# Layer 0 of a two-layer graph network for pairs of batches: a second level of seven-product blocking, and an order of all engines over two batches

## The chip, the core and the metric

The kernel runs on one core of one Trainium2 chip, in fp32 throughout. The time is the device time of one execution in microseconds (us); lower is better. A core has five engines with a queue each: TensorE (PE; its weight loads are PEld), VectorE (DVE), ScalarE (ACT), GpSimd (POOL) and SyncE (SP), which here issues nearly all DMAs.

## The reference

For each of 64 batches, x is 256 x 512 and adj is 256 x 256. Two layers follow each other, each with a residual and a layer norm:

```python
deg = jnp.sum(adj, axis=-1, keepdims=True)
agg = jnp.einsum('bij,bjf->bif', adj, x) / jnp.maximum(deg, EPS)
out = jnp.einsum('bnf,of->bno', jnp.concatenate([x, agg], axis=2), W)
x = _layernorm(x + relu(out))                          # layer 0
...
q, k, v = (proj(Wq, bq), proj(Wk, bk), proj(Wv, bv))   # 8 heads of 64
scores = einsum('bhqd,bhkd->bhqk', q, k) * SCALE * (adj + adj)[:, None]
ctx = einsum('bhqk,bhkd->bhqd', softmax(scores), v)
x = _layernorm(x + (ctx @ Wo.T + bo))                  # layer 1
```

## The kernel before, in words

**Seven products instead of eight.** The large products are done as 2 x 2 blocks by the Strassen-Winograd scheme. `winograd` (L408) makes the steps of one: products 5, 1, 3, 6, 2, 7, 4 into three PSUM accumulators a, b and c; "kept" steps that copy a partial sum out while the accumulator goes on accumulating; "joined" steps that add an accumulator to what was kept. The left blocks are sums of tokens that POOL makes (`token_sums`, L381), the right ones sums of weights made once at the start (`weights`, L239). So layer 0's product with both halves of W ("L": L1 to L7 are the products, Lk the copies on ACT at L464, Lj the joins on DVE at L429), Q and K together ("Q", L475 and L491), V ("V") and the output projection ("O"; keep_o, L516, adds `rest` on the way). L, V and O multiply at L448. A product of L is two fp32 matmuls of 128x128 weights and 512 columns: the 256 columns of both halves of W (m = 0 and 1), for two blocks of the contraction (c = 0 and 1). In the trace each fp32 matmul leaves two records.

**The stages of a batch.** x and adj come in turned layouts (Dzx, Dza) and as rows (Dx, Dadj). DVE transposes 32 x 32 blocks of the turned ones (xT0, xT1, aT; L354). L gives `oy`: half 0 is x W0, half 1 is x W1; then adj times half 1 by the seven-product scheme ("Y", lone 128x256 matmuls at L571, with aS and bS sums on POOL at L553), scaled by the degree and added (Yk, Yj; L593), relu and residual (AYr), layer norm (AYb on DVE, AYp on POOL, AYn on ACT). The result goes to DRAM (Dway), comes back turned (Dz1) and is transposed (x1T, L639), and once more as rows (`rest`, Drest) to which POOL adds the bias (bo).

**Attention.** For each of four pairs of heads a to d: scores (S, L674), multiplied by the mask by DVE from PSUM (m, L687), the row maximum (M, L697), exponential with the sum (e and f, ACT, L703), reciprocal (r), normalization (n, ACT, L720), a block transpose (T, DVE, L727), a way through DRAM (Dw, L732, into ws; Ds, L741, back into sT), contexts (C0a, C0b, C1a, C1b; L757), copies of them (c0, c1), O, and the last norm (lb, lp, ln) and output (Dout) from tile h1.

**Buffers.** SBUF tiles have one buffer each but for a few: zx, za and z (of step Dz1) are tiles of their own; sa to sd and sTa to sTd are eight tiles; xS, yS, cS, aS and yB hold four sums each. All PSUM accumulators rotate through eight banks of 128x512.

**The order.** Nothing is scheduled by a compiler: the steps are emitted in the order of three lists written out, START, PLAN and END, and every engine executes its own steps in that order. PLAN is one turn for one batch: "L1+2" is step L1 of the batch two ahead. Batches overlap over several turns.

## Time and profile before

| | |
|---|---|
| median of 3 runs | 3069.9 us (3069.35 to 3070.3) |
| the profiled execution | 3068.5 us, its span 3066.7 us, TensorE clock 0.998 |
| busy share of the span: PE, PEld, DVE, ACT, POOL | 99%, 76%, 70%, 55%, 42% |
| instructions: PE, DVE, ACT, POOL | 17552, 3914, 4995, 2189 |
| moved by DMA | 513.45 MB, 167 GB/s |

The span runs from the first to the last instruction of the execution that was profiled; the time beside it is that execution's own. A busy share is the part of the span in which at least one instruction of the engine was running; consecutive instructions overlap somewhat, so what one occupies is read from the distance between two starts. The row of a group of instructions gives busy time, mean duration, and what ended the idle time before it.

### The profile page before, as it was taken

How to read it: one execution, taken by the hardware profiler on the slowest of the kernel's cores; microseconds unless marked ns; L12 is line 12 of the kernel's file. 1: busy time of each engine (PE TensorE's matmuls, PEld its weight loads, DVE VectorE, ACT ScalarE, POOL GpSimd, SP SyncE). 2: the span in 40 equal slices, each digit the busy share in tenths (PEclk: the TensorE clock that was granted, in tenths of full speed). 3: DMA queues.
4: the chain of work that ended last, by engine and by line, in shares of the span. 5: the costliest groups of instructions: out<-in, count | busy, mean ns of one | idle time of the engine just before them, and what ended most of it. 6: DMA issues, size and time to landing. Idle time of an engine off the chain costs nothing.

```text
span 3066.7 us, 53019 instructions
## 1 busy us (share of the span) xinstructions
PE 3030.1 (99%) x17552; PEld 2323.7 (76%) x17552; DVE 2144.6 (70%) x3914; ACT 1689.7 (55%) x4995; POOL 1288.0 (42%) x2189
## 2 busy tenths in 40 slices
PE   7999999999999999999999999999999999999997
PEld 5778778777787787777877877778778777787785
DVE  5767777776777777777777677767776777676775
ACT  2655555555555556555555565555555555555565
POOL 4434444443444444434444444344444443444433
PEclk9999999999999999999999999999999999999999
DMA  8576566566675665665756656657666566576656
GB/s 175 134 183 177 154 179 175 152 183 166 158 182 153 178 172 154 179 168 155 186 152 178 172 154 177 173 151 185 159 172 172 155 182 171 151 184 162 165 144 173
DMA packets 494112, 513.45 MB, mean 167 GB/s; under 512 B 113808, under 2 KB 392336, under 8 KB 493840
## 3 DMA queue, kind: packets, MB, share of 16 engines
q1 hardware_dynamic: 493264, 509.02, 63.2%
q8 instruction: 141, 2.31, 0.3%
q10 hardware_dynamic: 576, 1.05, 0.1%
q14 instruction: 131, 1.07, 0.1%
HBM read 308.55 MB, written 201.33 MB: 166 GB/s over the span
## 4 chain that ended last, share of the span: by engine, by line
PE 97%; DMA 2%; DVE 1%; ACT 0%; SPq 0%; issue 0%; POOL 0%; POOLq 0%; DVEq 0%; ACTq 0%
PE Qa L475 15%; PE La L448 15%; PE Qc L475 7%; PE pc L757 7%; PE Oa L448 7%; PE Lc L448 7%; PE Va L448 7%; PE Qb L475 4%; PE Ya L571 4%; PE Lb L448 4%; PE Oc L448 4%; PE Vc L448 4%; PE Ycb L571 3%; PE scd L674 2%; PE Ob L448 2%; PE Vb L448 2%
## 5 line engine op out<-in xcount | busy, mean ns | idle before, releaser
L491 ACT ACTIVATE qk<-Qa,bqk 128x128 f32<-128x128 f32 x768 | 217.8, 364 | 518.3 <-PE Qa L475 518.3
L529 POOL TENSOR_SCALAR mv<-mv 128x1 f32<-128x1 f32 x256 | 76.9, 301 | 773.7 <-DVE mv L524 760.1
L464 ACT COPY oy<-La 128x512 f32<-128x512 f32 x192 | 112.6, 586 | 383.7 <-PE La L448 383.6
L389 POOL TENSOR_TENSOR yS<-x1T 128x256 f32<-128x256 f32 x128 | 94.2, 737 | 427.0 <-DVE x1T L639 426.3
L389 POOL TENSOR_TENSOR cS<-cT 128x256 f32<-128x256 f32 x128 | 90.9, 731 | 347.5 <-ACT cT L773 347.5
L516 DVE TENSOR_TENSOR h<-Oa,rest 128x256 f32<-128x256 f32 x192 | 81.5, 424 | 155.2 <-PE Oa L448 149.0
L720 ACT ACTIVATE sc<-sc,totalc 128x256 f32<-128x256 f32 x256 | 109.2, 498 | 106.4 <-DVE totalc L715 106.4
L653 POOL TENSOR_TENSOR rest<-rest,bo_sb 128x512 f32<-128x512 f32 x128 | 160.5, 1278 | 13.3 <-DMA rest<-way 13.3
L703 ACT ACTIVATE sd<-sd,nmaxd 128x256 f32<-128x256 f32 x256 | 127.0, 497 | 66.7 <-DVE nmaxd L697 66.7
L506 ACT COPY v<-Va 128x256 f32<-128x256 f32 x192 | 71.2, 371 | 158.2 <-PE Va L448 158.2
L727 DVE STREAM_TRANSPOSE sd<-sd 128x1024 f32<-128x1024 f32 x64 | 79.6, 1244 | 110.2 <-ACT sd L720 110.2
L530 POOL TENSOR_TENSOR mv<-mv,neg_half 128x1 f32<-128x1 f32 x256 | 144.9, 566 | 21.4
L553 POOL TENSOR_TENSOR yB<-oy 128x256 f32<-128x256 f32 x128 | 94.6, 739 | 131.7 <-DVE oy L429 126.4
L475 PEld LDWEIGHTS Qa<-x1T,Wq 128*128 128x128 f32 x1024 | 124.3, 192 | 28.2 <-issue 27.3
L429 DVE TENSOR_TENSOR oy<-Lb,oy 128x512 f32<-128x512 f32 x64 | 44.2, 690 | 141.9 <-PE Lb L448 135.2
L448 PE MATMUL Lb<-W,xT 128*128 128x512 f32 x256 | 122.2, 600 | 15.1 <-DMA W<-in_w0t_dram 15.1
L703 ACT ACTIVATE sa<-sa,nmaxa 128x256 f32<-128x256 f32 x256 | 127.0, 499 | 5.2 <-DVE nmaxa L697 5.2
L703 ACT ACTIVATE sb<-sb,nmaxb 128x256 f32<-128x256 f32 x256 | 126.3, 496 | 3.6 <-DVE nmaxb L697 3.6
L475 PEld LDWEIGHTS Qa<-x1T,Wq_sums 128*128 128x128 f32 x1024 | 124.2, 192 | 4.3 <-issue 1.1
L703 ACT ACTIVATE sc<-sc,nmaxc 128x256 f32<-128x256 f32 x256 | 126.4, 496 | 1.1 <-DVE nmaxc L697 1.1
L475 PEld LDWEIGHTS Qa<-yS,Wq 128*128 128x128 f32 x1024 | 124.2, 192 | 3.6 <-issue 0.5
L475 PEld LDWEIGHTS Qc<-yS,Wq_sums 128*128 128x128 f32 x1024 | 124.3, 192 | 3.3
(167 smaller groups left out, 8926.7 us busy)
## 6 DMA issues: line engine op xcount, KB each, us to landing
zx<-in_x_dram SPq DMA_DIRECT2D x256, 128.0 KB, 3.0
x<-in_x_dram SPq DMA_DIRECT2D x256, 128.0 KB, 3.5
way<-x SPq DMA_DIRECT2D x64, 512.0 KB, 3.2
z<-way SPq DMA_DIRECT2D x256, 128.0 KB, 2.8
rest<-way SPq DMA_DIRECT2D x64, 512.0 KB, 4.7
wsa<-sa SPq DMA_DIRECT2D x64, 512.0 KB, 5.6
wsc<-sc SPq DMA_DIRECT2D x64, 512.0 KB, 3.0
sTc<-wsc SPq DMA_DIRECT2D x256, 128.0 KB, 3.8
```

The costliest lines, as they stand in the source:

```text
L389: nc.gpsimd.tensor_tensor(part_of(s, b, [P, 4, 2, P])[:, k], left(b), right(b), op)
L448: nc.tensor.matmul(ps[:, :width].rearrange("p (m o) -> p m o", o=G), lhsT=left(k, b, c), rhs=w(WEIGHTS[k])[:, :, c], start=first and c == ...
L464: nc.scalar.copy(part_l(b, t, n), ps.rearrange("p (m o) -> p m o", m=2))
L475: nc.tensor.matmul(ps.rearrange("p (m j q) -> p m j q", m=2, j=2)[:, m, j], lhsT=wqk(WEIGHTS[k])[:, m, c, j * P : (j + 1) * P], rhs=left_y ...
L491: nc.scalar.activation(part_q(b, t, n)[:, m, j], ps.rearrange("p (m j q) -> p m j q", m=2, j=2)[:, m, j], AF.Identity, bias=bqk[:, m, c : ...
L530: nc.gpsimd.tensor_tensor(mv[:, 1:2], mv[:, 1:2], neg_half, ALU.pow)
L553: steps[f"{name}{k}"] = lambda b: nc.gpsimd.tensor_tensor(of(k)(b), left(b), right(b), op)
L571: nc.tensor.matmul(ps[:, G:] if acc == "b" else ps[:, :G], lhsT=left(b), rhs=right(b), start=k in (5, 1), stop=True, skip_group_check=True,)
L653: nc.gpsimd.tensor_tensor(rest, rest, bo_sb, ALU.add)
L703: nc.scalar.activation(rows(b)[:, r], rows(b)[:, r], AF.Exp, bias=of("nmax", b)[:, r : r + 1], accum_out=of("total", b)[:, r : r + 1],)
L720: nc.scalar.activation(rows(b)[:, r], rows(b)[:, r], AF.Identity, scale=of("total", b)[:, r : r + 1])
L757: nc.tensor.matmul(ps[j * D : (j + 1) * D, hp % 2], lhsT=held["v", b][:, c, h * D : (h + 1) * D], rhs=held[f"sT{name}", b][:, :, c, j * NT ...
```

## The change

- Layer 0 is done for two batches together. Each block product of L, except the second, becomes a 2 x 2 scheme of its own, over the two batches (beta), the two blocks of the contraction (c) and the two halves of W (m): seven unit products of 128x256 ("L51" is unit 1 of block product 5) instead of two times two matmuls of 512 columns. Product 2 stays as it was, once a batch (step L2).
- The left sides of the units are sums on POOL (Ls, four of 128x128 for each block product and pair), the right sides sums of weights made once (W0i, six times four sums of 128x256 on DVE).
- Each unit has its own "Le" step that takes its accumulator into `oy`: 42 a pair, of which eight are copies on ACT and 34 additions on DVE. The sums among the block products that accumulators held before are made by Lj2 and by La12 and La22, additions of 128x512 on POOL.
- The mask step m becomes four fused instructions that multiply and take the row maximum; M becomes a negation of four values on POOL.
- SBUF is rearranged: zx, za and z share one tile "z"; Ds brings the turned scores back into sa to sd themselves; `rest` serves in place of h1; chains of sums keep two tiles instead of four and overwrite the first; xT, oy, v and others have a tile for even and one for odd batches.
- START, PLAN and END are new; a turn is two batches. The start of PLAN, its middle, and the core of the rest of the diff:

```diff
+    Sa+0 Le62+2 Dx+2 Sb+0 Ls31+2 ma+0 La12+2 Sc+0 Dza+3 Sd+0 Ls72+2 mb+0 Ma+0 Ls74+2 fa+0 C1a-1 Ls33+2
+    C1b-1 mc+0 Mb+0 Ls32+2 Ls34+2 c1-1 L75+2 yS3+1 L71+2 fb+0 O2-1 Le71+2 cS1-1 Le75+2 L31+2 md+0 Mc+0
+    L76+2 bo-1 ec+0 L72+2 L73+2 O5-1 Le31+2 ea+0 Le76+2 L35+2 L36+2 Le35+2 cS2-1 O1-1 eb+0 Le36+2 cS3-1
+    Le73+2 L33+2 Ok1-1 L37+2 fc+0 Ok5-1 L77+2 Le37+2 O6-1 Ls41+2 Le33+2 Md+0 Le77+2 L32+2 yS1+1 ed+0
+    Le72+2 L45+2 rb+0 cS4-1 L74+2 Oj2-1 Y1+2 Ok6-1 aS1+2 rc+0 nb+0 L34+2 Le74+2 Ls43+2 O3-1 Le34+2 bS1+2
+    Le32+2 L42+2 La22+2 Oj3-1 O7-1 ra+0 lb0-1 na+0 Y5+2 bS3+2 Q5+1 Yk1+2 Tb+0 aS2+2 Ls42+2 fd+0 bS2+2
+    L41+2 Q1+1 Le41+2 La22+3 nc+0 Oj7-1 Ta+0 aS3+2 O4-1 Ls44+2 Yk5+2 Dwa+0 Y6+2 Qk1+1 Le45+2 Dwb+0 V5+1
...
+    AYr0+2 V6+1 AYb0+2 Q7+1 Vk5+1 yS4+1 Vk6+1 Dzx+4 Yk4+2 AYp0+2 AYr1+2 V7+1 Dsc+0 AYb1+2 aS3+3 AYn0+2
+    bS1+3 Q3+1 lb1-1 ln0-1 AYp1+2 Dsd+0 Qj7+1 V3+1 lp1-1 Le47+2 AYn1+2 Qj3+1 Q4+1 Vj3+1 Dway+2 ln1-1
+    Vj7+1 Dout-1 L44+2 Qk4+1 V4+1 Le44+2 xT0+4 Sa+1 Vk4+1 Qj2+1 Sb+1 xT1+4 Dz1+2 C0a+0 C1a+0 ma+1 C0b+0
+    Drest+0 C1b+0 c0+0 mb+1 Ma+1 c1+0 Sc+1 ea+1 cS1+0 Sd+1 mc+1 aS1+3 V2+1 fa+1 bS3+3 Mb+1 Y5+3 x1T+2
+    cS3+0 O2+0 eb+1 bS2+3 Y1+3 Dzx+5 O5+0 Mc+1 Yk1+3 aS2+3 fc+1 md+1 yS1+2 Q2+2 Dx+3 cS2+0 fb+1 Y6+3
+    Dadj+5 Y2+3 Yk6+3 aS4+3 ec+1 O1+0 Yk5+3 yS3+2 ra+1 Q5+2 Vj2+1 bo+0 Yj2+3 na+1 Y3+3 Y7+3 Yj3+3 Qk5+2
+    V5+2 bS4+3 rc+1 Ok5+0 xS1+4 Yj7+3 Q1+2 Ok1+0 nc+1 xS3+4 xT0+5 Oj2+0 O6+0 rb+1 Ta+1 V1+2 cS4+0 xT1+5
...
-FIRST_TURN = 3
-LAST_TURNS = 4
+FIRST_TURN = 2
+LAST_TURNS = 2
...
+    OUTER = {1: B11, 2: B21, 3: B22, 4: T4, 5: T1, 6: T2, 7: T3}
+    SPLIT = (1, 5, 6, 7, 3, 4)
+    w0_inner = const.tile([P, len(SPLIT), 3, G], F32, name="W0_inner")
+    def inner_weights(k):
+        unit = lambda c, m: w0(OUTER[k])[:, m, c]
+        t1, t2, t4 = (w0_inner[:, SPLIT.index(k), n] for n in range(3))
+        return {1: unit(0, 0), 2: unit(1, 0), 3: unit(1, 1), 4: t4, 5: t1, 6: t2, 7: unit(0, 1)}
+    def sum_inner_weights(k):
+        w = inner_weights(k)
+        @step(f"W0i{k}")
+        def _(_):
+            for dst, a, b in ((5, 7, 1), (6, 3, 5), (7, 3, 7), (4, 2, 6)):
+                nc.vector.tensor_tensor(w[dst], w[a], w[b], ALU.subtract)
...
+    def staged(name, b):
+        return part_of(name, b, [P, NT * F], tag="z")
...
-        z = tile_of("zx", b, [P, A, NT, F // A])
+        z = staged("zx", b).rearrange("p (b t k) -> p b t k", b=A, t=NT)
...
-        z = tile_of("za", b, [P, A, NT, N // A])
+        z = staged("za", b)[:, : NT * N].rearrange("p (b t k) -> p b t k", b=A, t=NT)
...
+    def x_turned(b):
+        return part_of("xT", b, [P, FC, NT, P], tag=f"xT{b % 2}")
...
+    def chain_sums(s, engine, place, block):
+        def put(k, left, right, op):
+            steps[f"{s}{k}"] = lambda b: engine.tensor_tensor(place(b, k == 3), left(b), right(b), op)
+        put(1, lambda b: block(b, 1, 0), lambda b: block(b, 1, 1), ALU.add)
+        put(2, lambda b: place(b, 0), lambda b: block(b, 0, 0), ALU.subtract)
+        put(3, lambda b: block(b, 0, 0), lambda b: block(b, 1, 0), ALU.subtract)
+        put(4, lambda b: block(b, 0, 1), lambda b: place(b, 0), ALU.subtract)
...
+        def place(b, n):
+            return part_of(s, b, [P, 2, 2, P])[:, n]
+        chain_sums(s, nc.gpsimd, place, block)
+        return lambda k, b, c: (block(b, *BLOCK[k]) if k in BLOCK else place(b, k == 7))[:, c]
...
-    def part_l(b, t, n):
-        return part_of("oy", b, [P, 2, NT, F])[:, :, t, n * G : (n + 1) * G]
-    def keep_l(b, ps, t, n):
-        nc.scalar.copy(part_l(b, t, n), ps.rearrange("p (m o) -> p m o", m=2))
-    winograd("L", right_weights(token_sums("xS", "xT"), w0, F), keep_l, part_l)
+    def oy_block(b, m, t, n):
+        return part_of("oy", b, [P, 2, NT, F], tag=f"oy{b % 2}")[:, m, t, n * G : (n + 1) * G]
...
+    def x_sum(b, n):
+        return part_of("xS", b - b % 2, [P, 2, 2, 2, P])[:, n, b % 2]
+    chain_sums("xS", nc.gpsimd, x_sum, x_block)
+    def split_product(k):
+        def unit(b, beta, c):
+            return (x_block(b + beta, *BLOCK[k]) if k in BLOCK else x_sum(b + beta, k == 7))[:, c]
+        def unit_sum(b, n):
+            return part_of(f"xs{k}", b, [P, 4, P], tag=f"xs{SPLIT.index(k) % 2}")[:, n - 1]
+        for n, left, right, op in (
+            (1, lambda b: unit(b, 1, 0), lambda b: unit(b, 1, 1), ALU.add),
+            (2, lambda b: unit_sum(b, 1), lambda b: unit(b, 0, 0), ALU.subtract),
+            (3, lambda b: unit(b, 0, 0), lambda b: unit(b, 1, 0), ALU.subtract),
+            (4, lambda b: unit(b, 0, 1), lambda b: unit_sum(b, 2), ALU.subtract),
+        ):
+            small_sum(f"Ls{k}", n, lambda n: lambda b: unit_sum(b, n), left, right, op)
+        w = inner_weights(k)
+        lefts = {q: lambda b, q=q: unit(b, *BLOCK[q]) for q in BLOCK}
+        lefts |= {q: lambda b, n=n: unit_sum(b, n) for q, n in ((5, 1), (6, 2), (7, 3), (3, 4))}
+        def accumulator(q, b):
+            name = f"L{k}a" if q in (1, 6, 7, 4) else f"L{k}cb"
+            ps = bank(name, b) if (name, b) not in held else held[name, b]
+            return ps[:, G:] if q == 2 else ps[:, :G]
+        def product(q):
+            @step(f"L{k}{q}")
+            def _(b):
+                nc.tensor.matmul(
+                    accumulator(q, b), lhsT=lefts[q](b), rhs=w[q], start=q in (5, 1), stop=True, skip_group_check=True
+                )
+        t, n = {5: (1, 1), 3: (0, 1)}.get(k, (1, 0))
+        def taken(q, beta, m):
+            @step(f"Le{k}{q}")
+            def _(b):
+                dst, ps = oy_block(b + beta, m, t, n), accumulator(q, b)
+                if k in (1, 5) and q in (5, 1, 6, 4):
+                    nc.scalar.copy(dst, ps)
+                else:
+                    nc.vector.tensor_tensor(dst, ps, dst, ALU.add)
+        for q in (5, 1, 3, 6, 2, 7, 4):
+            product(q)
+        for q, beta, m in ((5, 1, 1), (1, 0, 0), (6, 0, 1), (4, 1, 0), (3, 0, 1), (2, 0, 0), (7, 1, 1)):
+            taken(q, beta, m)
...
+    def both(b, t, n):
+        oy_block(b, 0, t, n)
+        return held["oy", b][:, :, t, n * G : (n + 1) * G]
+    @step("L2")
+    def _(b):
+        ps = bank("L2", b).rearrange("p (m o) -> p m o", m=2)
+        for c in range(2):
+            nc.tensor.matmul(ps, lhsT=x_block(b, 0, 1)[:, c], rhs=w0(B21)[:, :, c], start=c == 0, stop=c == 1)
+    @step("Lj2")
+    def _(b):
+        ps = held["L2", b].rearrange("p (m o) -> p m o", m=2)
+        nc.vector.tensor_tensor(both(b, 0, 0), ps, both(b, 1, 0), ALU.add)
+    @step("La12")
+    def _(b):
+        nc.gpsimd.tensor_tensor(both(b, 0, 1), both(b, 1, 0), both(b, 1, 1), ALU.add)
+    @step("La22")
+    def _(b):
+        nc.gpsimd.tensor_tensor(both(b, 1, 1), both(b, 1, 1), both(b, 1, 0), ALU.add)
...
-        return part_of("h1", b, [P, NT, F])[:, t, n * G : (n + 1) * G]
+        return held["rest", b][:, t, n * G : (n + 1) * G]
     def keep_o(b, ps, t, n):
-        rest = held["rest", b][:, t, n * G : (n + 1) * G]
-        nc.vector.tensor_tensor(part_o(b, t, n), ps[:, :G], rest, ALU.add)
+        nc.vector.tensor_tensor(part_o(b, t, n), ps[:, :G], part_o(b, t, n), ALU.add)
...
-        return lambda b: part_of("yB", b, [P, 4, G])[:, k - 1]
+        return lambda b: part_of("yB", b, [P, 2, G])[:, k == 3]
...
-        z = tile_of("z1", b, [P, NT, A, P])
+        z = staged("z1", b).rearrange("p (t b k) -> p t b k", t=NT, b=A)
...
-            tile_of(f"s{name}", b, [P, A, NT, R, L])
+            s = tile_of(f"s{name}", b, [P, A, NT, R, L])
+            nmax = tile_of(f"nmax{name}", b, [P, R], small, "nmax")
             for j in range(2):
-                nc.vector.tensor_tensor(
-                    rows(b)[:, j * NT : (j + 1) * NT],
-                    sc(b, j).rearrange("p t (k l) -> p t k l", l=L),
-                    held["adj", b].rearrange("p t (k l) -> p t k l", l=L),
-                    ALU.mult,
-                )
+                for t in range(NT):
+                    r = j * NT + t
+                    nc.vector.tensor_tensor_reduce(
+                        out=s[:, :, :, r],
+                        in0=sc(b, j)[:, t].rearrange("p (a c l) -> p a c l", a=A, l=L),
+                        in1=held["adj", b][:, t].rearrange("p (a c l) -> p a c l", a=A, l=L),
+                        scale=1.0,
+                        scalar=-3.4028234663852886e38,
+                        op0=ALU.mult,
+                        op1=ALU.max,
+                        accum_out=nmax[:, r : r + 1],
+                    )
         @step(f"M{name}")
         def _(b):
-            nmax = tile_of(f"nmax{name}", b, [P, R], small, "nmax")
-            nc.vector.tensor_reduce(nmax, rows(b), AX.XY, ALU.max, negate=True)
+            nc.gpsimd.tensor_scalar(of("nmax", b), of("nmax", b), -1.0, None, ALU.mult)
...
-            sT = tile_of(f"sT{name}", b, [P, A, NT, R, L])
             for a, part in groups():
                 nc.sync.dma_start(
-                    out=sT[part].rearrange("l b c r m -> l b (c r m)"),
+                    out=of("s", b)[part].rearrange("l b c r m -> l b (c r m)"),
...
-    turn = [(name[:-2], int(name[-2:])) for name in PLAN.split()]
...
-        for i in range(FIRST_TURN, B - LAST_TURNS):
+        for i in range(FIRST_TURN, B // 2 - LAST_TURNS):
             for name, ahead in turn:
-                run(name, i + ahead)
+                run(name, 2 * i + ahead)
```

## The prediction

> **What bounds the kernel now.** I read the page first: busy time by engine and the shares of the chain that ended last.
>
> ```profile
> PE 3030.1 (99%) x17552; PEld 2323.7 (76%) x17552; DVE 2144.6 (70%) x3914; ACT 1689.7 (55%) x4995; POOL 1288.0 (42%) x2189
> PE 97%; DMA 2%; DVE 1%; ACT 0%; SPq 0%; issue 0%; POOL 0%; POOLq 0%; DVEq 0%; ACTq 0%
> ```
>
> TensorE is on the chain for 97% of the span. To see whether it ever waits in the steady part, the view of waits on PE from 200 to 2866 us, which has two rows in all:
>
> ```profile
> PE pc L757 <- DMA sTb<-wsb: 1.3, 1, 1.3
> PE pc L757 <- DMA sTd<-wsd: 0.6, 1, 0.6
> ```
>
> So 1.9 us in 2666: any TensorE time taken out is time saved, as long as no other engine becomes late. The cycle of one batch, from one start of the scores of heads d to the next, is a row of the view of busy time by stretch (sum columns PE, PEld, DVE, ACT, POOL):
>
> ```profile
> 1526.41:1573.49 47.08, 47.08 (x275) 36.26 (x274) 33.27 (x62) 26.32 (x78) 19.90 (x35) 1.00 0.61 166
> ```
>
> A pair of batches is 94.16 us of TensorE; beside it DVE has 66.5 us of work, ACT 52.6, POOL 39.8. What an instruction occupies is read from starts, not durations, since matmuls overlap. PE's timeline:
>
> ```profile
> 1514.48 0.59 PE L571 MATMUL Ya<-yB,aS 128*128 128x256 f32 x2
> 1514.91 0.59 PE L571 MATMUL Ycb<-oy,aS 128*128 128x256 f32 x2
> 1515.34 1.03 PE L448 MATMUL Vc<-Wv_sums,yS 128*128 128x256 f32 x4
> ...
> 2897.42 1.88 PE L448 MATMUL Lc<-W_sums,xS 128*128 128x512 f32 x4
> 2899.13 1.88 PE L448 MATMUL La<-W_sums,xS 128*128 128x512 f32 x4
> ```
>
> A lone 128x256 product (two records) takes 0.433 us, with weights of its own and a semaphore of its own; a block product of layer 0 (two of 128x512) takes 1.717. The same way: a Q product 1.785, a V or O product 0.865, four scores or contexts 0.865. DVE's timeline gives its spacing:
>
> ```profile
> 1501.58 0.41 DVE L516 TENSOR_TENSOR h<-Oc,rest 128x256 f32<-128x256 f32 x1
> 1501.91 0.41 DVE L429 TENSOR_TENSOR h<-Ob,h 128x256 f32<-128x256 f32 x1
> 1502.24 0.17 DVE L715 RECIPROCAL totala<-totala 128x4 f32<-128x4 f32 x1
> ...
> 1531.23 1.28 DVE L687 TENSOR_TENSOR sa<-sca,adj 128x512 f32<-128x512 f32 x2
> 1532.42 1.27 DVE L687 TENSOR_TENSOR sb<-scb,adj 128x512 f32<-128x512 f32 x2
> ...
> 1533.73 1.22 DVE L697 TENSOR_REDUCE nmaxb<-sb 128x4 f32<-128x1024 f32 x1
> 1534.87 1.21 DVE L697 TENSOR_REDUCE nmaxa<-sa 128x4 f32<-128x1024 f32 x1
> ```
>
> 128x256 with a PSUM operand: 0.335. Two of 128x512: 1.20, so 0.60 each and 1.03 ns per further element. The reduction: 1.14.
>
> **The Trainium skill.** "Perfetto Trace Analysis", Identifying the Most-Contended Engine: matmul busy share is no measure of how near TensorE is to its limit; weight-load share is better. Here the two are 99% and 76%; I therefore rest on start-to-start times and on the absence of waits. "TensorE: Matmul & The Clock Gate", step by step: the next weights load while a matmul runs. The trace agrees at 256 columns: lone Y products follow at 0.433 us, half of the 0.865 of a pair. "VectorE: DVE Perf Modes", Two Vector instructions with no wait between them: an op that also writes out its accumulator is two instructions, the op and a read. No DVE row of before has one; ACT's exponential has (below). "GPSIMD Engine Reference", Specifications: GpSimd shares its SBUF interfaces with VectorE when that has two SBUF inputs. The new DVE sums have one input in PSUM, and POOL's 128x256 sums at 0.73 to 0.74 us in busy stretches show no scatter to speak of.
>
> **The change part by part, for a pair of batches.**
>
> *TensorE, layer 0.* Removed: 14 block products x 1.717 = 24.04. Added: 6 x 7 = 42 unit products x 0.433 = 18.19, and product 2 of both batches, 2 x 1.717 = 3.43. Net -2.42. I do not charge for weights, as said.
>
> *TensorE, the order.* A cycle's products sum to 7 x 1.717 + 7 x 1.785 + 14 x 0.865 + 7 x 0.433 + 8 x 0.865 = 46.58; the cycle is 47.08. The 0.50 belongs to the three changes between full tiles, scores (64 rows) and contexts (64 columns): 0.17 each. The new order changes four times in each half of a turn (contexts 0, scores, contexts 1, then full; and scores a, b, four contexts, scores c, d, full): 8 against 6, +0.33. TensorE: -2.09 a pair, x 32 = -66.9.
>
> *DVE.* Removed: eight mask products x 1.20 = 9.6; eight reductions x 1.14 = 9.1; four joins of layer 0 (Lj3, Lj7) x 0.60 = 2.4; in all 21.1. Added: of 42 "Le" steps 8 go to ACT, 34 x 0.335 = 11.4. Then 32 fused mask-and-maximum ops (TTR), an operation that no row shows. The nearest is the 128x256 product, 0.335. For the accumulator read, ACT:
>
> ```profile
> 1541.46 0.49 ACT L703 ACTIVATE sb<-sb,nmaxb 128x256 f32<-128x256 f32 x1
> 1541.86 0.19 ACT L703 ACTIVATION_READ_ACCUMULATOR sb<-sb,nmaxb 128x1 f32 x1
> 1541.95 0.49 ACT L703 ACTIVATE sb<-sb,nmaxb 128x256 f32<-128x256 f32 x1
> ```
>
> The read adds 0.09. Low: 0.335 + 0.07 (two reciprocals start 0.07 apart) = 0.41. High: two cycles an element, 0.335 + 0.265 + 0.11 = 0.71. I take 0.45 since the op has the same two inputs as the product it replaces: 14.4. DVE: 66.5 - 21.1 + 11.4 + 14.4 = 71.2 of a pair of about 92 us, 77%; at 0.71 it is 79.5, 86%. A gain there buys nothing, DVE being off the path.
>
> *POOL.* 24 sums of 128x128 x 0.465 = 11.2, four 128x512 sums (La12, La22) x 1.28 = 5.1, eight negations x 0.3 = 2.4: 39.8 to 58.5, 64%. The negation now stands between mask and exponential, where the wait is POOL's queue: at most one running sum, 1.28. *ACT.* Eight copies of 0.50 go, eight of 0.3 come: nothing.
>
> *Buffers.* sa..sd now take the place of sTa..sTd: a batch's mask step waits for the last batch's contexts, and contexts come some 8.5 us of TensorE after the issue of Dsd (second half: V3, Q4, L44, V4, scores a and b, three contexts = 0.87 + 1.79 + 0.43 + 0.87 + 5 x 0.93 = 8.6). The landing takes 3.0 by the page. Covered, with 5 us to spare. zx, za and z share one tile: each load waits on SP for the transpose before it, and the loads behind it too. Smallest room I find: Dz1 after xT1 of the next pair, then eight score and context groups, V2 and Y5 until x1T, 8.7 us against 2.8 of landing. h1 is now rest itself: Drest waits for Dout, 2.3 to land, with about 6 us between. The token, adjacency and y sums keep two tiles instead of four, the second and fourth sum written over the first: yS2 on POOL now waits until Q5 and V5 are done. Behind it in POOL's queue stand bS4 and the norm factors, for which Y4 and ACT wait. From V5 to Q6, which needs yS2, the list has V1 and six units and Y products, 0.87 + 6 x 0.433 = 3.5 us, against 0.74 and a sum before it. All at nothing; without this cover, see the last rival.
>
> *Stalls in the turn.* At its start the list gives DVE ma, mb, mc and then Le71, for which L76 waits. TensorE reaches L76 after 4 x 0.93 + 2 x 0.93 + 2 x 0.433 + 0.865 + 0.433 = 7.75. DVE is done at 0.93 + 0.2 + 12 x 0.45 + 0.335 + 0.15 = 7.0. Close. I put 0.2 us a pair for such places: +6.
>
> *Start.* 24 weight sums x 0.335 = 8 us of DVE, among the first pair's Le steps: for blocks 6, 7, 3, 4 DVE has 7 x 0.335 + 4 x 0.335 = 3.7 against 3.03 of TensorE, +2.7. Larger: batch 0's Y used to end at 33.3 us and x1T could have been there at about 48 (way issued at 39.6, z at 42.4 to 43.8, 2.9 to land, transpose 1.2); 18 us of batch 1's products filled that. Now both batches' layer 0 comes before, and what is left is 8 Y products, the bias product 3.5 and two units: 7.4 against 15, so +7.6. With 2.7 for the second x behind the first transpose and smaller waits: +13. *End.* Before, scores of batch 63 began (3004.2) before contexts of 62 (3021.9). In place they can't, but 24.6 us of O, Q and V now stand behind scores 62. I take +6, from -3 to +15.
>
> **Sum**, against the profiled execution's own 3068.5 us: - 66.9 + 6 + 13 + 6 = 3026.6. The median of the runs is 1.4 above that execution: 3028.
>
> **The rivals.**
>
> *The ends and stalls cost nothing* (covered after all): 3068.5 - 66.9 + 1.4 = 3003. For it: 1.9 us of waits in the steady part of before. Against: the 15 us chain at the start is there in any order. 12%.
>
> *The fused op is dear, and the kernel slower.* Place: DVE's queue after the scores. At 0.71, Le71 ends at 1.13 + 8.52 + 0.485 = 10.1, so L76 waits 2.4. In the second half Y6 is reached after 8 x 0.93 + 0.865 x 3 + 0.433 x 2 = 10.9, and needs ma, mb, mc (from 2.99), x1T 1.16, Yk1 0.54: 13.2, so 2.3. 4.7 a pair, x 32 = 150 in place of 6: 3172. It decides from a stall of 1.5 a pair, which is 0.75 in each place, 12 ops each: from about 0.58 us an op. Against: same inputs as the product; for: no row shows it. 11%.
>
> *The shared buffers.* The round trip of s or of z comes late, because SP's queue holds a load behind a waiting one. Against: 5 us to spare. For: SP waits already now, 390 us for xT in the steady part. At 0.5 us a batch 3060, at 1 us 3092. 17%: 6% still faster, 4% the same, 7% slower.
>
> *That TensorE doesn't shorten* because weight loads show is excluded by the lone Y products.
>
> **How the numbers follow.** Forecast 3028 (3012 to 3050) 60%; cover holds 12%; dear op 11%; buffers 17%. Measurement of this kernel can tell about 0.2%, 6 us. Faster 60 + 12 + 6 = 78%, same 4%, slower 11 + 7 = 18%. The range leaves out the dear op, the worst of the buffers and the lowest of the first rival: 2998 to 3078.
>
> **What would show it.** Two-batch cycle at 92 us; unit products 0.433 apart; TTR with its read under 0.5; no repeated wait of PE on Le or on s; TensorE idle before the first Q by some 8 us. Wrong if L76 or Y6 waits for DVE in every turn, if contexts wait for s, or if the end is longer by over 15 us.

## The result, and the profile after

The kernel is slower: 3089.6 us (3087.0 to 3092.6), 1.0066 times the 3069.6 us of the kernel before (95% interval 1.0048 to 1.0083). The forecast was 3028, its range 2998 to 3078. The profiled execution took 3087.0 us, its span is 3085.2. A cycle below is that of two batches, the mean over 24 turns, taken from the starts of the scores of heads d on TensorE.

The page of the changed kernel, busy time and the chain that ended last:

```profile
PE 2995.2 (97%) x18704; PEld 2534.1 (82%) x18704; DVE 2246.7 (73%) x6178; ACT 1652.9 (54%) x4995; POOL 1853.6 (60%) x3341
PE 81%; DMA 11%; DVE 3%; SPq 2%; issue 1%; POOL 1%; ACT 0%; DVEq 0%; POOLq 0%; ACTq 0%
```

TensorE is busy for 35 us less than before (2995.2 against 3030.1): the products did shrink. But the chain is no longer TensorE's alone: DMA went from 2% to 11% of it. Where TensorE waits, the view of waits from 200 to 2866 us says; before the change this view had two rows, 1.9 us in all:

```profile
PE Qb L621 <- DVE x1T L778: 15.9, 25, 1.5
PE pc L901 <- DMA sc<-wsc: 5.1, 5, 2.2
PE L6cb L547 <- DVE oy L560: 4.8, 27, 0.2
PE pc L901 <- DMA sd<-wsd: 4.7, 10, 1.5
```

Columns: total us, times, longest. It is 30.5 us, and each wait costs some 0.16 us more than the view shows: the contexts of sd in the turn below wait 0.48 us and start 0.64 us later than the spacing of their neighbours would have them. The first row comes in 25 turns, always at Q2+2 in the middle of the turn. The view by stretch, one turn (sum columns PE, PEld, DVE, ACT, POOL):

```profile
1092.97:1186.63 93.66, 92.77 (x586) 78.97 (x584) 69.34 (x192) 51.61 (x157) 57.46 (x105) 1.00 0.64 169
```

The cycle of two batches is 93.80 us in the mean, from 93.17 to 94.30; before it was 94.17, always within 0.01. The forecast said 92.3. DVE's timeline shows the fused operation:

```profile
1088.75 0.40 DVE L829 CUSTOM_DVE_ANT_0 sa<-sca,adj 128x256 f32<-128x256 f32 x1
1089.08 0.08 DVE L829 DVE_READ_ACCUMULATOR2_ANT nmaxa<- 128x1 f32 x1
1089.08 0.42 DVE L829 CUSTOM_DVE_ANT_0 sa<-sca,adj 128x256 f32<-128x256 f32 x1
1089.42 0.08 DVE L829 DVE_READ_ACCUMULATOR2_ANT nmaxa<- 128x1 f32 x1
1089.42 0.42 DVE L829 CUSTOM_DVE_ANT_0 sa<-sca,adj 128x256 f32<-128x256 f32 x1
```

One every 0.345 us, its accumulator read included: hardly more than the plain 128x256 product (0.335).

**Where the time went.** Two parts. Over the 28 turns: 28 x (93.80 - 94.17) = -10.4, where the forecast had 28 x -1.89 = -52.9. What is left of the execution, START and END with four pairs: 3087.0 - 28 x 93.80 = 460.6 against 3068.5 - 28 x 94.17 = 431.7, so +28.9, where the forecast had 13 + 6 - 4 x 1.89 = +11.4. -10.4 + 28.9 = +18.5, the difference of the two executions. 42.5 us of the error lie in the turns, 17.5 at the ends.

**Why x1T is late.** SP's timeline (issue times of the DMAs of the middle of one turn; x4 are four transfers of 128 KB):

```profile
1160.90 0.34 SPq L877 DMA_DIRECT2D wsa<-sa  x1
1161.28 0.43 SPq L877 DMA_DIRECT2D wsb<-sb  x1
1166.91 0.32 SPq L877 DMA_DIRECT2D wsc<-sc  x1
1167.34 2.20 SPq L885 DMA_DIRECT2D sb<-wsb  x4
1169.64 0.38 SPq L877 DMA_DIRECT2D wsd<-sd  x1
1170.06 2.57 SPq L885 DMA_DIRECT2D sa<-wsa  x4
1172.73 1.88 SPq L372 DMA_DIRECT2D zx<-in_x_dram  x4
1174.73 2.03 SPq L885 DMA_DIRECT2D sc<-wsc  x4
1177.23 2.19 SPq L885 DMA_DIRECT2D sd<-wsd  x4
1179.83 0.38 SPq L765 DMA_DIRECT2D way<-x  x1
1180.37 2.88 SPq L940 DMA_DIRECT2D out_dram<-rest  x4
1185.87 1.79 SPq L771 DMA_DIRECT2D z<-way  x4
```

The stores of sa and sb leave at 1161; by the page they land in 2.7 and 3.6 us, so from 1165 both could be loaded back. But the list puts the store of sc next, and that one waits on SP for a transpose that DVE ends at 1166.9. Behind it 21 transfers stand ahead of way, which leaves at 1179.83.

Nor does SP get through these as fast as it can issue. By the trace no more than eight transfers are under way at any time: none of the 2961 that follow the first eight is issued before the one eight places ahead of it has landed, and 755 are issued within 0.12 us of that landing (263 before the change). In the turn shown, the first quarter of sd leaves at 1177.23, zx's first quarter having landed at 1177.17, and way at 1179.83, sc's first quarter having landed at 1179.76. SP's own view of waits from 200 to 2866 us has such waits, for data that the waiting transfer does not use (L885 loads s, L765 stores way):

```profile
SPq L885 <- DMA zx<-in_x_dram: 37.3, 104, 0.9
SPq L765 <- DMA sc<-wsc: 7.0, 25, 0.4
```

Between the store of sc and way they come to 2.2 us a turn (the median of 24 turns). ACT's timeline says when way's data were ready:

```profile
1176.29 0.81 ACT L678 ACTIVATE x<-oy,mv 128x512 f32<-128x512 f32 x1 [0.92 <-POOL mv L674]
```

1177.10: way leaves 2.7 us late in this turn, 3.3 in the median; z then waits for way to land, x1T for z, Q2+2 for x1T (0.32 us in this turn, 0.64 in the mean). sd is loaded at 1177 to 1179.4, and its contexts, at 1184.65, wait 0.48 for it. The Trainium skill, "DMA: Bandwidth & Descriptors", Anatomy of one DMA: DMA engines don't wait on semaphores; any wait is made by the issuing sequencer ahead of dispatch. The trace agrees: a store that waited for DVE held two loads whose data had landed.

### The profile page after: what moved, and what is told of

It is laid out like the page before. It is cut to its first block, busy times and chain, and to the rows that moved or that the text cites. A ratio compares the mean times of both kernels' runs of the same rounds, so it can differ in the third digit from the quotient of the medians.

```text
span 3085.2 us, 60241 instructions
## 1 busy us (share of the span) xinstructions
PE 2995.2 (97%) x18704; PEld 2534.1 (82%) x18704; DVE 2246.7 (73%) x6178; ACT 1652.9 (54%) x4995; POOL 1853.6 (60%) x3341
## 4 chain that ended last, share of the span: by engine, by line
PE 81%; DMA 11%; DVE 3%; SPq 2%; issue 1%; POOL 1%; ACT 0%; DVEq 0%; POOLq 0%; ACTq 0%
PE Qa L621 13%; PE Oa L494 7%; PE Qc L621 7%; PE Va L494 6%; PE pc L901 5%; PE L L599 3%; PE Qb L621 3%; PE Ya L710 3%; PE Vc L494 3%; PE Oc L494 3%; DMA way<-x 3%; DMA sc<-wsc 2%; PE Ycb L710 2%; DMA z<-way 2%; PE L7a L547 2%; PE L3a L547 2%
## 5 line engine op out<-in xcount | busy, mean ns | idle before, releaser
L917 ACT COPY cT<-pc 128x512 f32<-128x512 f32 x128 | 75.0, 586 | 432.3 <-PE pc L901 432.3
L678 ACT ACTIVATE x<-oy,mv 128x512 f32<-128x512 f32 x128 | 103.5, 812 | 118.0 <-POOL mv L674 87.8
L865 ACT ACTIVATE sd<-sd,totald 128x256 f32<-128x256 f32 x256 | 109.2, 498 | 102.4 <-DVE totald L860 102.4
L732 DVE SCALAR_TENSOR_TENSOR oy<-Ya,deg,oy 128x256 f32<-128x256 f32 x256 | 120.2, 470 | 59.6 <-PE Ya L710 59.4
L865 ACT ACTIVATE sa<-sa,totala 128x256 f32<-128x256 f32 x256 | 109.2, 498 | 94.5 <-DVE totala L860 94.4
L621 PEld LDWEIGHTS Qb<-x1T,Wq 128*128 128x128 f32 x1024 | 121.9, 192 | 30.0 <-DVE x1T L778 27.9
L621 PE MATMUL Qb<-x1T,Wq 128*128 128x128 f32 x1024 | 127.7, 278 | 16.8 <-DVE x1T L778 16.6
L599 PE MATMUL L<-W,xT 128*128 128x512 f32 x256 | 121.5, 599 | 16.1 <-DMA W<-in_w0t_dram 16.1
L829 DVE CUSTOM_DVE_ANT_0 sa<-sca,adj 128x256 f32<-128x256 f32 x256 | 93.2, 420 | 55.6 <-PE sca L813 30.0
L568 POOL TENSOR_TENSOR xs<-xS 128x128 f32<-128x128 f32 x256 | 125.6, 497 | 7.5 <-PE L5cb L547 2.8
```

The source lines that it names most:

```text
L568: steps[f"{name}{k}"] = lambda b: nc.gpsimd.tensor_tensor(of(k)(b), left(b), right(b), op)
L599: nc.tensor.matmul(ps, lhsT=x_block(b, 0, 1)[:, c], rhs=w0(B21)[:, :, c], start=c == 0, stop=c == 1)
L621: nc.tensor.matmul(ps.rearrange("p (m j q) -> p m j q", m=2, j=2)[:, m, j], lhsT=wqk(OUTER[k])[:, m, c, j * P : (j + 1) * P], rhs=left_y(k ...
L865: nc.scalar.activation(rows(b)[:, r], rows(b)[:, r], AF.Identity, scale=of("total", b)[:, r : r + 1])
```

## The experiments

First theory: what is late is late because of the order on SP's queue. Rivals: the transfers are slow because too many go at once; the shared tile z; DVE; and for the ends, the number of small sums at the start.

**e1, the store alone moved.** This kernel stores the second half of the even batch's x ahead of its norm, so it leaves that norm out of what follows.

```diff
- ... AYp1+2 Dsd+0 Qj7+1 V3+1 lp1-1 Le47+2 AYn1+2 Qj3+1 Q4+1 Vj3+1 Dway+2 ...
+ ... AYp1+2 Dway+2 Dsd+0 Qj7+1 V3+1 lp1-1 Le47+2 AYn1+2 Qj3+1 Q4+1 Vj3+1 ...
```

> Edit: in the turn's list the store Dway+2 stands ahead of the load Dsd+0 in place of nine engine steps behind it. Theory (SP's queue): x of the even batch is ready at 1083.3 us in the cycle looked at, but its store leaves at 1087.4, behind the loads of sc and sd, the latter waiting for its own store to land; so z, x1T and with them Q2+2 come late (15.9 us of waits in 25 of 28 turns, and some 0.16 us of drain at each). With the store ahead, x1T is there 1.5 to 3 us earlier, the wait is gone: 20 us less than the changed kernel, less up to 8 us for sd coming 0.4 us later; 3070 to 3078. Rival (the landings of way and z, now 4.5 and 3.8 us against 3.2 and 2.8, take what the store gains, or Dz1 waits for the transposes that free the shared tile z): the wait on x1T stays at 10 us or more and the time at 3085 to 3092.

3130.1 us, 1.0206 (1.018 to 1.0232); waits on sd 32.2 us and on x1T 30.2. Not a test of either theory, since the norm, now behind the store, can only write x when that has read it. It shows one thing: with the store just ahead of it, sd comes late (28 waits, where the changed kernel has 10).

**e2, z1 out of the shared tile.** z1 gets a tile that it shares only with the sums yS, which are made after z1 has been transposed. To make room, the small tiles `deg` and `stats` get other numbers of buffers, five and one.

```diff
-        z = staged("z1", b).rearrange("p (t b k) -> p t b k", t=NT, b=A)
+        z = tile_of("z1", b, [P, NT * F], tag="yS").rearrange("p (t b k) -> p t b k", t=NT, b=A)
```

> Edit: the turned x1 (z1) does not share the tile z with zx and za any more; it shares one with the sums yS, which are made only after z1 has been transposed. Nothing else is moved. Rival (the shared tile z holds Dz1 up): the wait of Q2+2 on x1T goes, 15 to 20 us less than the changed kernel, 3068 to 3074. Theory (SP's order of issue holds it up, Dz1 waits for the way store to land at 1092.0 us where the transposes that free z are done at 1088.8): no change within 4 us, 3085 to 3094, and the wait on x1T stays at 12 to 20 us.

3085.5 us, 1.0052 (1.0037 to 1.0067), cycle 93.61. The wait on x1T is 8.6 us in 20 turns, less than expected, but e4, whose turns are those of the changed kernel, has 9.8 in 20 turns and a cycle of 93.65: within the spread. The shared tile isn't the cause; e9 below, where it stays shared and the waits go, says the same.

**e3, Le65 ahead of L62.**

```diff
- L65+4 Le67+4 L62+4 Le65+4
+ L65+4 Le67+4 Le65+4 L62+4
```

> Edit: the addition Le65+4 stands ahead of the unit product L62+4, in place of behind it; both use the same PSUM bank. Theory: Le65 waits for L62 only because of its place in the list, and L63, which needs the bank's first half back, waits 0.18 us for Le65 in each turn, and the pair of stretches around it is 0.34 us over its nominal time; the wait goes: 28 x 0.34 = 9.5 us less than the changed kernel, 3077 to 3083. Rival (DVE has other work just then, Lj2+5 and Le67, and is simply late): Le65 comes no earlier and the time stays at 3085 to 3092.

3100.9 us, 1.0101 (1.0083 to 1.0118), against both. The row of the waits:

```profile
PE L6cb L542 <- DVE oy L555: 16.6, 27, 0.6
```

Now L62 waits 0.6 us a turn, where L63 waited 0.18. L62 writes the other half of the bank than the one that Le65 reads: in this program the two halves of a bank are not independent. The Trainium skill, "PSUM — Partial Sum Buffer", PSUM bank collisions raise a hardware error: guard by bank and quadrant, not by address. The kernel's semaphores do that, and so the place in the list decides which of two steps in different halves waits.

**e4, whole blocks for the first two batches.** START begins with batch 0's and then batch 1's whole block products:

```diff
- ... L2:0 W0s1:0 W0s2:0 xT0:1 xT1:1 L2:1 W0i1:0 xS1:1 Dza:0 Ls53:0 L51:0 Ls51:0 ...
+ ... P2:0 W0s1:0 W0s2:0 Wb:0 P1:0 W0s4:0 P5:0 Pk1:0 xS2:0 aT:0 Pj2:0 Dzx:1 aS1:0 P6:0 ...
```

> Edit: the first two batches get whole block products of layer 0 (P1 to P7, as before the change, batch 0 complete ahead of batch 1); the weight sums of the inner scheme move behind the first Q. From the third batch on nothing is changed. Theory (the start is set by POOL's and DVE's small sums: PE lacks 23.5 us of its nominal work up to 260 us where before it lacked 7.8, waiting for yB, oy, xs, aS, and its clock is 0.91 to 0.96 from 20 to 100 us): 2.4 us more of products, and 10 to 18 us less in all than the changed kernel, 3070 to 3080; TensorE's clock at 20 to 100 us back to 0.98 or more. Rival (the start costs what it does because the first batch's round trip through DRAM is late in any order, or because the later start-up steps are the slow ones): within 5 us of the changed kernel.

3081.3 us, 1.0034 (1.0023 to 1.0046), just above the range that I had given. By its own trace most of that is not the start: 3081.2 - 28 x 93.65 = 459.0 against 460.6. The theory fell in this form. POOL's and DVE's sums hold TensorE less (yB and aS 1.1 us in all up to 260 us, 8.2 in the changed kernel), but my list holds it instead: 4.0 us for Wo, which I had put late, and 1.9 that the view puts down to the scaling of a weight on ACT. e11 moves both. Its wait for Wo is gone; the 1.9 us are still there, now put down to a copy on ACT, so the scaling was not their cause. TensorE's clock from 20 to 100 us is 0.96, where I had expected 0.98 or more.

**e5, norm and store ahead of the load of sd.**

```diff
- ... AYp1+2 Dsd+0 Qj7+1 V3+1 lp1-1 Le47+2 AYn1+2 Qj3+1 Q4+1 Vj3+1 Dway+2 ...
+ ... AYp1+2 AYn1+2 Dway+2 Dsd+0 Qj7+1 V3+1 lp1-1 Le47+2 Qj3+1 Q4+1 Vj3+1 ...
```

> Edit: the norm AYn1+2 and the store Dway+2 both stand ahead of the load Dsd+0 (the run with the store alone stored the second half of x ahead of its norm, so it is no test). Theory (SP's queue holds the store behind the load of sd, which waits for its own store): way leaves 2 to 3 us earlier, Dz1+2 follows after the output's store, x1T is there ahead of Q2+2: waits on x1T in the steady part under 3 us in place of 15.9; the cycle of two batches 0.4 to 0.7 us shorter; 3072 to 3081. Rival (landings and other transfers take it back, sd comes late instead): waits on x1T 8 us or more, or waits on sd of over 15 us, and the time at 3084 to 3092.

3094.8 us, 1.008 (1.0067 to 1.0092), cycle 94.01. The waits:

```profile
PE pc L897 <- DMA sd<-wsd: 31.2, 26, 1.6
PE L6cb L543 <- DVE oy L556: 4.8, 27, 0.2
```

No wait on x1T is left in any turn, as the theory had it, but sd now comes 1.2 us late in 26 turns, and that is the rival's case, with a time 3 us above its range. The two loads and the store want the same moment of SP's queue; swapping them only changes which is late.

**e6, the L6 units in another order.**

```diff
- L66+4 V2+2 Le66+4 Lj2+5 L67+4 Dsd+1 L65+4 Le67+4 L62+4 Le65+4 L64+4 x1T+3 L63+4
+ L66+4 L65+4 L62+4 Le66+4 Lj2+5 Le65+4 L67+4 V2+2 Le67+4 Dsd+1 L64+4 x1T+3 L63+4
```

> Edit: units L65 and L62 stand ahead of V2+2, and V2+2 between L67 and L64, so that a V product lies between each unit and the addition that must clear its half of the bank. Theory (a unit that writes either half of a bank waits for a read of either half that is listed ahead of it, and the other way round; moving Le65 alone only moved the wait to L62 and lengthened it to 0.6 us): no wait on Le65 is left, 0.3 to 0.4 us less in each of 28 turns, 9 to 11 us less than the changed kernel: 3076 to 3083. Rival (DVE is late there whatever the order): a wait of 0.2 us or more on an addition stays in each turn and the time at 3086 to 3092.

3086.9 us, 1.0065 (1.0051 to 1.0078), cycle 93.77. The wait on Le65 is gone from the view, the time is not: sc waits 9.3 us where it waited 5.1. TensorE seems to have reached the next late transfer sooner; e11 tests that.

**e7 and e8, half the batches.** `B = 32` in place of the batches of x.

> The changed kernel with the loops cut to the first 32 batches; the other 32 rows of the output are left out. Theory (0.4 us gained a pair in the steady part, some 32 us lost at the ends): 16 pairs of 93.75 less than 3087 to 3092, so 1587 to 1592, which is 25 to 30 us more than the kernel before cut in the same way. Rival (the loss lies in the steady part, and the ends cost only the 19 us that were forecast): 1575 to 1582.

> The kernel before with the loops cut to the first 32 batches; the other 32 rows of the output are left out. 3069.6 less 16 pairs of 94.17: 1562.9, within 2.

1588.0 and 1564.3 us. Twelve turns taken off: 1588.0 - 12 x 93.80 = 462.4 and 1564.3 - 12 x 94.17 = 434.3; the ends cost 28.1 us more than before, as in the full runs (28.9). So the split between turns and ends holds, as far as one run of each can say.

**e9, the loads of sa and sb ahead of the store of sc.**

```diff
- Dwb+0 ... Tc+0 Q6+1 Vk1+1 Yj2+2 Dwc+0 Td+0 Dsb+0 Y4+2 Qk6+1 Q2+1 aT+3 Dwd+0 Qk5+1 Dsa+0
+ Dwb+0 ... Tc+0 Q6+1 Vk1+1 Yj2+2 Dsa+0 Dsb+0 Dwc+0 Td+0 Y4+2 Qk6+1 Q2+1 aT+3 Dwd+0 Qk5+1
```

> Edit: the loads Dsa+0 and Dsb+0 stand ahead of the store Dwc+0, in place of behind it and behind Dwd+0 and Dzx+4; SP and the DMA engines do nothing then for some 5 us (share 0.02 from 1063 to 1068 us), while from 1078 to 1088 they are at 1.08 and 1.14. Theory (a crowd of transfers at the end of each half: sa, sb, sc, sd, zx, way, output, z, rest, 0.5 MB each; whichever stands first is in time, and the others late): with two of them moved into the idle stretch sc and sd land 2 to 3 us earlier and way leaves 2 us earlier; the waits on sc, sd and x1T fall from 26 to under 8 us in all, 17 to 27 us less than the changed kernel: 3062 to 3072. Rival (not the crowd, but the chain of norm, store, load and transpose of x1T sets the wait): only sc and sd gain, the wait on x1T stays at 10 us or more, 3079 to 3088.

3052.7 us, 0.9941 (0.9928 to 0.9955): 37 us less than the changed kernel and faster than the kernel before, by moving two words; I had expected 17 to 27. SP's timeline in the middle of a turn:

```profile
1057.39 0.34 SPq L872 DMA_DIRECT2D wsa<-sa  x1
1057.78 0.43 SPq L872 DMA_DIRECT2D wsb<-sb  x1
1060.08 1.76 SPq L880 DMA_DIRECT2D sa<-wsa  x4
1061.95 1.79 SPq L880 DMA_DIRECT2D sb<-wsb  x4
1063.84 0.38 SPq L872 DMA_DIRECT2D wsc<-sc  x1
1064.93 0.34 SPq L872 DMA_DIRECT2D wsd<-sd  x1
1065.81 2.58 SPq L367 DMA_DIRECT2D zx<-in_x_dram  x4
1068.49 1.81 SPq L880 DMA_DIRECT2D sc<-wsc  x4
1070.44 3.23 SPq L880 DMA_DIRECT2D sd<-wsd  x4
1073.77 0.38 SPq L760 DMA_DIRECT2D way<-x  x1
...
1079.23 1.79 SPq L766 DMA_DIRECT2D z<-way  x4
```

The loads fill the pause in which SP waited. To compare, take each kernel's start of scores b on TensorE as zero (1180.40 and 1076.90): way leaves at -3.1 in place of -0.6, with x ready at -3.3 in both; z at +2.3 in place of +5.5; sd's load at -6.5 in place of -3.2. In the median of 24 turns way leaves 0.03 us behind x, where it was 3.3. Between the store of sc and way stand 13 transfers instead of 21, and their waits for the one eight places ahead come to 1.0 us in place of 2.2. The waits from 200 to 2866 us that come in every turn:

```profile
PE L6cb L542 <- DVE oy L555: 4.8, 27, 0.2
```

and the cycle, 92.47 in all but one of 24 turns:

```profile
1082.43:1174.90 92.47, 92.29 (x586) 79.03 (x584) 69.48 (x192) 51.61 (x157) 57.48 (x105) 1.00 0.65 171
```

28 x (93.80 - 92.48) = 37.0, the whole gain. The transfers themselves are no quicker: way and z land in 4.6 and 3.9 us by its page, 4.5 and 3.8 in the changed kernel. They are begun sooner.

**e10, the output's store behind z's load as well.**

```diff
- Dway+2 ln1-1 Vj7+1 Dout-1 L44+2 ... xT1+4 Dz1+2 C0a+0
+ Dway+2 ln1-1 Vj7+1 L44+2 ... xT1+4 Dz1+2 Dout-1 C0a+0
```

> Edit: as the run with sa and sb loaded earlier, and the output's store Dout-1 stands behind Dz1+2, no longer between Dway+2 and Dz1+2. Theory (crowd): way and z land in 3.5 us or less where they took 4.5 and 3.8, nothing waits for x1T; 0 to 8 us less than the run without this move: 3058 to 3070. Rival: the output's store now goes beside z and rest and bo, O and the last norm come late: 3070 or more.

3052.8 us, 0.9944 (0.9931 to 0.9956), cycle 92.50, way and z in 4.3 and 3.9 us: no effect. That the output beside way stretches it, as the theory of the crowd had it, is not supported.

**e11, all moves:** e10, e6's order, and e4's start with Wo loaded right behind Wv and the scaling of Wq behind Pk4:1.

> Edit: the two moves of transfers, the order of the L6 units, and whole blocks for the first two batches with Wo and the scaling of Wq placed so that PE does not wait for them. Theory: the moves of transfers as above, L6 another 9 us in the steady part once transfers no longer take its gain, and the start 5 to 12 us: 3040 to 3058, faster than the kernel before. Rival (a wait that goes comes back at the next late transfer, as it did in the two runs before): 3066 to 3080.

3040.5 us, 0.9905 (0.9891 to 0.9918), cycle 92.35. No wait of every turn is left in the view. The L6 order is now worth 28 x 0.15 = 4 us, not 9: of the 0.42 us a turn that L63's wait costs in e9, 0.28 come back behind V2, where L64 has to wait until Le67 has read its accumulator (in one turn Le67 ends at 1206.19 and L64 starts at 1206.25). The view doesn't show that wait. The ends: 3039.7 - 28 x 92.35 = 453.9, against 462.3 in e9, so the start gives 8 us.

**e12, one change of kind less in a turn.** To e11, with START and END to match:

```diff
- PLAN: ... C1a-1 Ls33+2 C1b-1 mc+0 ... c1-1 ... (next turn, behind the scores)
- ... Dout+0 L66+4 ... Dsd+1 L64+4 ... C0b+1 Le64+4 Le63+4 La12+5 Drest+1 Vj2+2 c0+1
+ ... L66+4 ... Dsd+1 Dout+0 L64+4 ... C0b+1 Le64+4 Le63+4 C1a+1 La12+5 C1b+1 Drest+1 Vj2+2 c0+1 c1+1
```

> Edit: as the run with all moves, and the contexts C1a and C1b of the odd batch stand ahead of the next scores, so that the turn changes seven times between full tiles, scores and contexts in place of eight; Dout+0 behind Dsd+1. Theory: 0.2 us a turn less, 28 turns: 4 to 7 us less than the run with all moves, if sd lands in time. Rival (sd+1 lands too late for it): waits of 0.5 us or more on sd in each turn, 10 us or more above the run with all moves.

3070.7 us, 1.0 (0.9992 to 1.0008). The rival: TensorE waits 22.6 us for sd, in 23 turns. The change saved, some 0.2 us, is small beside a load that is asked for 1 us too soon.

**e13, the changed kernel without the output's stores in the turns.**

```diff
- Dout-1   (and)   Dout+0
```

> The changed kernel without Dout in the turn's list: the output's stores are left out for the batches of the 28 turns, so their rows stay unwritten. Each half of a turn has 0.5 MB less to move just where way, z and rest go. Theory (SP's order: way leaves behind the loads of sc and sd, 4 us after x is ready, and none of this is taken out): the wait on x1T stays at 8 us or more in the steady part and the time at 3078 or more. Rival (crowd: landings of 4.5 and 3.8 us are long because the output moves beside them): way and z land in 3.5 and 3.2 us or less, the wait on x1T is gone, 3050 to 3068.

3088.0 us, 1.0062 (1.0047 to 1.0077), cycle 93.73; x1T 10.6 us in 19 turns; way and z land in 4.5 and 3.8. Half a megabyte less in each half of a turn changes nothing: the output, which stands behind way in the list, is not the cause. With e9 this settles where the steady loss comes from: from what SP has to get through ahead of way and sd. Two things stay open. e9 took eight transfers out of that stretch as well as changing the order, so what the limit of eight under way costs by itself was not tested. Nor was why way lands in 5.0 us in this half of a turn (the median), in 3.0 in the other and in 3.2 before the change.

**e14, mask and maximum apart again,** on e9 (the two products and the reduction of the kernel before).

> Edit: the run with sa and sb loaded earlier, with the mask and the maximum of the kernel before (two products of 128x512 at 0.60 and a reduction at 1.14, 2.34 us for a pair of heads, in place of four fused operations at 0.345, 1.38 us); the negation goes back into the reduction. DVE has 7.7 us more in a turn. Theory (DVE is off the path: before Le71 now stand three masks and two maxima, 5.9 us, where the forecast had 5.4 and TensorE came to L76 later than that): no change to 15 us more than the run with sa and sb loaded earlier, 3050 to 3067. Rival (0.585 us a row, at the point from which the forecast's dear op decides): L76 or Y6 waits 0.7 us or more in each turn, 20 to 50 us more, 3072 to 3102.

3080.8 us, 1.004 (1.0026 to 1.0054): 28 us more than e9, cycle 93.18. The time is the rival's (20 to 50), not the theory's (0 to 15), though the steps that wait are others than it named. PE's timeline, and then DVE's:

```profile
1057.50 0.59 PE L542 MATMUL L3cb<-W,xS 128*128 128x256 f32 x2
1057.93 0.59 PE L542 MATMUL L4cb<-W_inner,xs 128*128 128x256 f32 x2
1058.67 0.70 PE L542 MATMUL L7a<-W_inner,xS 128*128 128x256 f32 x2
1059.20 0.60 PE L705 MATMUL Ya<-oy,aT 128*128 128x256 f32 x2
```

```profile
1057.08 1.21 DVE L831 TENSOR_REDUCE nmaxd<-sd 128x4 f32<-128x1024 f32 x1
1058.20 0.41 DVE L555 TENSOR_TENSOR oy<-L7a,oy 128x256 f32<-128x256 f32 x1
```

L74 must wait until Le77 has read its accumulator; Le77 stands behind the last reduction and starts at 1058.20. L74 (the third line) would have followed L45 (the second) after 0.433 us, at 1058.37, 0.3 us sooner. Y1 behind it loses another 0.10. L36, which waits for Le31 behind the reduction for heads c, loses 0.15 and the product behind it 0.10. That makes nearly all of the 0.70 a turn, and the ends take 9 us more. So DVE is close behind the path after all, and the fused operation is worth about 28 us in this order. The view of waits shows none of it: TensorE's modelled busy time covers such short delays, only its starts tell.

**e15, the end of e11.**

```diff
- Dwc:1 ... Dwb:1 Oj3:2 Dsa:1 ... Dsc:1 ... Dwd:1 Dout:2 C0a:1 Dsb:1 C1a:1 Dsd:1
+ Dsa:1 Dwc:1 ... Dwb:1 Oj3:2 ... Dsc:1 ... Dsb:1 Dwd:1 Dsd:1 Dout:2 C0a:1 C1a:1
```

> Edit: the run with all moves; in the list of the end the last batch's load of sa goes ahead of its store of sc, that of sb ahead of the store of sd, and the output of the batch before behind the load of sd. Theory (same cause as in the turns: sa's data lie ready at 2995 us and the load leaves at 3000 behind two stores that wait for transposes; PE waits 3.3 for sa and 4.0 for sb, its clock at 0.73): 3 to 6 us less than the run with all moves, 3034 to 3038. Rival (the end is bound by the chain of softmax and O itself): within 1.5 us of it.

3037.0 us, 0.9894 (0.9879 to 0.9909), 3.6 us less than e11, 2.6 if each is set against the runs of the kernel before that go with it. The intervals of the two ratios overlap, but the traces agree: from the scores of heads d of batch 60 on, e15 takes 160.9 us and e11 164.4. So the theory holds, and the cause is the one in the turns. The contexts of the last batch still wait 2.3 us for sc and 3.5 for sd. This is the fastest version.

## Why the prediction was wrong, point by point

- *TensorE, layer 0, -2.42 a pair.* Right. Summed from the spacing of its starts, a pair's products fell from 93.09 to 90.59 us, -2.50; units follow at 0.43.
- *Changes of kind, +0.33.* About right. What lies over the products is 1.08 us a pair before, for six changes; in e9 it is 1.89, of which 0.42 belong to L63's wait (below) and 1.47 to eight changes. That is 0.18 each in both kernels, and +0.39.
- *The fused operation, 0.45, bounds 0.41 to 0.71.* It takes 0.345, below my low end; I had added the read as if it had its own time. DVE has 69.3 us in a turn, POOL 57.5, as forecast (71.2 and 58.5). "A gain there buys nothing" was wrong: e14.
- *Buffers, all at nothing.* This is the step that failed. Its numbers: "Covered, with 5 us to spare" for s, and 8.7 us against 2.8 of landing for z. Both were counted from a place in the list to the use, with landings of the kernel before. But a DMA starts when SP reaches it, not at its place: in the even batches' half of a turn sd's load left 1.7 to 3.4 us ahead of scores b, behind a load of zx and two stores that wait for transposes, and SP issues each only once the one eight places ahead has landed, which I hadn't looked for. And sd lands in 4.5 us by the page where my working had 3.0; both are figures of one of four parts. From the first issue to the last landing the four took 4.4 us before and take 6.4 in this half (medians). For z I named the transposes xT as what holds Dz1; they end at 1181.1 in the turn shown, z leaves at 1185.87, held by way's landing. I looked at the last buffer to come free and not at the last event. It cost 1.32 us a turn, 37 in all (e9).
- *The rival of shared buffers*, 17%, was right in its mechanism ("SP's queue holds a load behind a waiting one") and its size, 0.66 us a batch, lies between its two cases. That z or s are shared is not the reason, however: z1 out of the shared tile changed nothing (e2), and in e9 both stay shared and the waits go.
- *Stalls, 0.2 a pair, L76 on Le71.* No such wait. L63 on Le65 comes instead, 0.34 us with its restart and 0.08 behind it: Le65 stands behind L62, which writes the other half of the same bank, a dependence that I hadn't looked for.
- *Start +13, end +6.* The start is the second term that was too small; the end was about right. By the starts of its products TensorE loses 35.6 us over their nominal spacing up to the scores of heads d of batch 4, against 11.3 before. The first matmul is 1 us later, and the first turn takes 101.0 us, 7 more than the mean: its contexts wait 3.7 us for sc and sd, and behind that the granted clock is 0.50 from 295.5 to 302 us. That makes some +32. From the scores of heads d of batch 60 on it is 25.0 against 19.6, +5. Less some 9 us that the products at the two ends save, that is the 28.9. The first Q was not delayed by one wait of 8 us, as forecast: TensorE waits in a dozen places for POOL and DVE, 4.5 us for yB the longest, with DVE busy for 35.8 of the 40 us up to 60. Of the 17.5 us that were not forecast 8 come back in e11 and 3 in e15; the other 6 or so are not settled.
- *The other rivals.* That the ends and stalls cost nothing, and that the fused operation is dear, are both refuted above.
- *The sum.* 3028 + 37 (transfers) + 17.5 (ends) + 28 x (92.48 - 92.28) = 5.6 (products and changes nearly cancel; L63's wait of 0.42 stands in place of the 0.2 for stalls) = 3088.

## What to carry to other kernels

Where one engine issues all DMAs in order, follow that queue as you follow TensorE's: for each transfer, which waiting one stands ahead of it, and where the queue idles while landed data wait to be fetched. Look in the trace for how many can be under way at once, too: in this program the ninth waits for the first to land, so a slow landing delays transfers that have nothing to do with it. Room for a buffer is counted from the moment of issue to the use, and for a chain of store, load and transpose from the event that comes last, not from the one that the change makes you think of. If a shortened engine gains less than its products, look for a wait that comes in nearly every period with a scattered length; moving one step past another only moves it, as long as the queue between stays full.

## What was not expected of the hardware

TensorE runs slower after a pause of 3 to 4 us. At the end of e11:

```profile
2999.68 1.03 PE L483 MATMUL Oa<-Wo,cS 128*128 128x256 f32 x4
3001.22 1.13 PE L483 MATMUL Oa<-Wo_sums,cT 128*128 128x256 f32 x4 [0.52 <-DVE rest L464]
3005.61 1.84 PE L890 MATMUL pc<-sa,v 128*64 128x256 f32 x8 [3.26 <-DMA sa<-wsa]
...
3018.88 2.07 PE L483 MATMUL Ob<-Wo,cT 128*128 128x256 f32 x4 [0.68 <-ACT cT L906]
...
3027.29 1.03 PE L483 MATMUL Oc<-Wo,cS 128*128 128x256 f32 x4
```

A context (8 records) takes 1.84 us in place of 1.03 to 1.08, an O product 2.07 in place of 1.03; the granted clock is 0.73 from 3000 to 3020 us. By stretches (the clock is the third figure from the end):

```profile
3005.80:3009.20 3.40, 3.03 (x16) 1.47 (x13) 0.00 (x0) 0.12 (x1) 0.00 (x0) 0.50 1.04 322
3012.70:3022.80 10.10, 7.87 (x25) 4.86 (x26) 0.00 (x0) 1.17 (x2) 3.16 (x3) 0.50 0.37 86
```

Between the two, and from 3022.9 on, it is 1.00. The six groups from 3005 to 3022 take 11.5 us where at full clock they would take 6.3, so two waits of 3.3 and 4.0 us cost 5 us more than themselves. The Trainium skill, "TensorE: Matmul & The Clock Gate", Part 1, says that the clock halves after an idle window of some 3.4 us and returns after as long a busy one. The trace agrees with the halving, behind the pauses of 3.3 and 4.0 us, and the first time with the return, after 3.4 us. The second time the clock came back only after 10 us, though TensorE worked from 3013.6 on with pauses of no more than 0.7 us. The start of the changed kernel shows the same more faintly, 0.96 of the clock from 20 to 60 us and 0.91 from 60 to 100, where the kernel before kept 1.00.
